# Four post-norm layers on one core: separate buffers and PSUM for the last mixer's layers, one buffer set for the third mixer's second half, one matmul pair per tile and weight pieces by block for the further tiles

## The chip, the core and the metric

The kernel is one program on one core of a Trainium2 chip. Engines: TensorE (PE; its weight loads are shown as PEld), VectorE (DVE), ScalarE (ACT), GpSimd (POOL) and SyncE (SP). Each runs its own instructions strictly in order and waits on semaphores of the others. SP, ACT and POOL also start DMA transfers; POOL alone starts the indirect ones here, in which a list of row numbers says where each of 128 rows goes or comes from. The metric is device time in microseconds (us) of one execution; "before" is the median of four runs.

## What is computed

2048 tokens (8 sequences of 256) of 128 numbers go through four layers. Each layer is a mixer and a feed-forward part (FFN), each added to its input and normalised (post-norm), in float32:

```
x = norm(x + mixer_k(x));  x = norm(x + ffn_k(x))        k = 0..3
mixer 0  recurrent scan over time          ffn 0  8 experts, 2 per token
mixer 1  latent attention, 64 latents      ffn 1  64 experts, 6 per token, and a shared one
mixer 2  gated linear attention, 4 heads   ffn 2  160 experts, 8 per token, and a shared one
mixer 3  6 layers of linear attention      ffn 3  attention with projections
         and a leaky feed-forward                 of four widths
```

Two parts matter here. Mixer 2, for each head: with c the running sum of the log gate z, o = (q k^T * exp(c_t - c_s) for s <= t) v, then a norm, a gate and a projection. FFN 2 for a token t and its eight chosen experts e, with shares p:

```
y[t] = sum over e of p[t,e] * ( silu(x[t] @ w_gate[e]) @ w_down[e] )      w_gate: 128x64, w_down: 64x128
```

## The kernel before

**Groups, halves, lanes.** The tokens are four groups g of 512 tokens. Groups 0 and 1 are the first half, 2 and 3 the second. `lanes[0]` and `lanes[1]` each own two of the eight PSUM banks (`ps`) and small buffers; group g uses lane g % 2. The expert code has the other four banks, `ps_m` (2) for gates and transposes, `ps_o` (2) for results.

**What sets the order.** The program is written stage by stage, half by half, but a tile scheduler with a timeline simulation orders the instructions of every engine: an instruction may move ahead of others of the text if its operands and buffers are free, and the queues are then fixed. Buffers come from pools; a tile with a tag has as many buffers as its pool or its `bufs` says, and a new tile of the tag waits until the oldest is no longer read. Memory of a closed pool is used again, and its new owner waits for the last reader of the old one.

**FFN 2 by tiles of 64 rows.** For one half, `plan()` turns the counts of tokens per expert into row numbers (`pl`). Each expert owns one tile of 64 rows; tokens beyond 64 go to further tiles. `place()` (L475) scatters: for each group, 4 x 8 indirect DMAs of 128 token rows from SBUF into the DRAM array `placed`, 64 per half. `routed_experts()` then works through 36 blocks of eight tiles: 20 own blocks, whose weights SP loads from the input, and 16 further blocks, whose weights first have to be laid out in the DRAM array `further`. That is done in 16 pieces: POOL gathers 128 rows of the weights into a tile `got` (L446; two buffers), SP writes it to a slice of `further`. Every further block reads a part of all 16 slices. For each block SP loads the rows (`xb`, L525) and the weights (`w`), PE transposes xb (L128), multiplies by the gate (L553), ACT and DVE apply silu (L557, L558), PE multiplies by the down weights (L571), ACT copies to `ob` and writes it to the DRAM array `made`. `xb` and `w` have two buffers. An own tile has one gate and one down matmul; in a further block both have two, with halves of the weights. `gather()` (L590) brings the rows back with 64 indirect DMAs per half, and DVE adds them, times the token's share (L487 computes the shares, inside `place()`).

**The stages in the text.** `stage(run, route, half)` runs a mixer and the routing of the next FFN for both groups of a half. Around the change the text reads:

```
stage(run, l2_route, first); plan(first); l1_experts(second)
routed_experts(first); stage(run, l2_route, second); gathers(first); plan(second)
es.close(); layers = l3_attn(ctx); run = layers(first)
routed_experts(second); gathers(second)
```

`run()` after that executes the six layers of mixer 3 for the first half, then FFN 3 for it, then both for the second half. `l2_attn` (L804) has a set of working buffers per lane. `l3_attn` (L913) loads the weights of all six layers at once (`w = [[load(...)]...]`, L917); its buffers use the memory that mixer 2's pools give back at `es.close()`. Its `layer()` has the projections L941 and L956, the attention L976 to L991 and the leaky feed-forward L1000 to L1006. One group in one of its six layers is called a group-layer here; there are 24. The memsets at L1044 to L1050 prepare tiles of FFN 3 on POOL.

## Time and profile before

| | us |
|---|---|
| median of four runs | 2382.15 |
| the four runs | 2385.47, 2378.82, 2386.44, 2376.43 |
| the profiled execution | 2375.16 |
| its span (first to last instruction) | 2373.4 |
| PE busy in it | 1836.8 |
| DVE, ACT, POOL busy | 1272.9, 958.4, 288.8 |
| mean granted PE clock | 0.83 |

The profile is of one execution. A page gives busy times by engine, the span in 40 slices (one slice is 59.3 us; each digit is the busy share in tenths), the chain of work that ended last, and groups of instructions by line. A window row gives the same for a chosen stretch: from, to, length, then the busy time and the number of instructions of PE, PEld, DVE, ACT and POOL, the granted PE clock, the busy share of the 16 DMA engines, and GB/s. A timeline row is one instruction or several of one kind: start, duration, engine, line, operation, output <- input, number, and in brackets how long the engine was idle before it and what ended that. Stages in the span: up to 980 us layers 0 and 1; to 1130 the first scatter, beside the second half of FFN 1; to 1435 the first half's blocks and the second half's mixer 2, with the second scatter from 1315; to 1548 the first gather; to 1762 the second half's blocks and the first layers of mixer 3; to 1860 the second gather; to 2373 the rest of mixer 3 and FFN 3.

### The profile page before, as it was taken

The page shows a single profiled execution, that of the slowest core. Times are in us where ns is not written, and L with a number is a line of the kernel's source. Part 1 is how long each engine was busy: PE and PEld are TensorE (multiplying, and loading weights), DVE is VectorE, ACT ScalarE, POOL GpSimd, SP SyncE. Part 2 cuts the span into 40 slices and gives each one's busy share as a digit, 9 for nine tenths or more (in the row PEclk, how much of TensorE's full clock was granted, in tenths as well). Part 3 has the DMA queues.
Part 4 walks back from the last instruction along what each step waited for, and adds up shares of the span by engine and source line. Part 5 has one row for each costly group of instructions (what it writes and reads, how often), then busy time and mean ns, then how long its engine had stood idle before and what let it go on. Part 6 is the DMA issues. An engine that isn't in the chain of part 4 may idle for free.

```text
span 2373.4 us, 48482 instructions
## 1 busy us (share of the span) xinstructions
PE 1836.8 (77%) x19224; PEld 1207.6 (51%) x19224; DVE 1272.9 (54%) x4476; ACT 958.4 (40%) x2417; POOL 288.8 (12%) x307
## 2 busy tenths in 40 slices
PE   5888879978999999846897221476774799998787
PEld 4666644544555456312585121354652566565554
DVE  3000055777877667823467221366554788566644
ACT  5667643724654365201433000143441454434413
POOL 1000000000000000172100635511025200000000
PEclk8676669989999999967799555589886899889858
DMA  2000029602324423532676243487531000000000
GB/s 85 5 4 5 5 92 274 191 11 58 96 76 116 122 63 84 171 115 86 233 221 214 91 131 123 131 273 257 177 111 39 19 1 1 1 5 5 1 1 10
DMA packets 169123, 219.78 MB, mean 93 GB/s; under 512 B 19104, under 2 KB 114848, under 8 KB 168896
## 3 DMA queue, kind: packets, MB, share of 16 engines
q1 hardware_dynamic: 145728, 164.23, 23.3%
q0 software_dynamic: 12800, 33.57, 4.6%
q10 hardware_dynamic: 10368, 18.88, 2.1%
q8 instruction: 151, 2.47, 0.4%
q14 instruction: 76, 0.62, 0.1%
HBM read 152.07 MB, written 64.55 MB: 91 GB/s over the span
## 4 chain that ended last, share of the span: by engine, by line
PE 53%; DVE 13%; DMA 9%; ACT 9%; another core or an unknown queue 7%; issue 7%; SPq 1%; POOL 1%; ACTq 0%; DVEq 0%; POOLq 0%
PE ps_o L301 6%; PE ps_m L306 6%; ACT st L248 4%; PE ps_s L239 4%; PE ps_m L311 4%; PE ps L128 3%; DMA got<-in_F_w_dram,ei 3%; PE ps L1006 2%; DMA w<-further 2%; PE ps L1000 2%; DMA further<-got 2%; PE ps_m L553 2%; PE ps L1126 2%; PE ps_s L224 2%
## 5 line engine op out<-in xcount | busy, mean ns | idle before, releaser
L308 ACT ACTIVATE h<-ps_m 128x512 f32<-128x512 f32 x196 | 116.0, 597 | 317.7 <-PE ps_m L306 211.2
L239 PE MATMUL ps_s<-st,L_a 128*32 128x16 f32 x8160 | 200.8, 206 | 44.0 <-ACT st L248 22.3
L248 ACT ACTIVATE st<-ps_s 64x32 f32<-64x32 f32 x1024 | 195.7, 191 | 90.9 <-PE ps_s L239 54.5
L301 PE MATMUL ps_o<-h,wd 128*128 128x512 f32 x384 | 206.0, 622 | 23.3 <-DVE h L314 13.2
L306 PE MATMUL ps_m<-xT,wg 128*128 128x512 f32 x384 | 203.4, 613 | 12.1 <-ACT h L308 8.7
L239 PEld LDWEIGHTS ps_s<-st,L_a 128*32 128x32 f32 x8160 | 158.1, 134 | 88.7 <-ACT st L248 73.6
L311 PE MATMUL ps_m<-xT,wu 128*128 128x512 f32 x256 | 140.6, 632 | 39.9 <-DVE junk L487 20.0
L446 POOL DMA_INDIRECT got<-in_F_w_dram,ei x32 | 31.7, 990 | 1121.9 <-DVE ei L435 969.7
L314 DVE TENSOR_TENSOR h<-h,bc 128x512 f32<-128x512 f32 x192 | 131.8, 689 | 58.7 <-ACT h L308 40.1
L571 PE MATMUL ps_o<-w,h 64*64 64x64 f32 (+1 forms) x1664 | 79.7, 274 | 104.8 <-issue 67.1
L269 DVE SCALAR_TENSOR_TENSOR outsT<-xnT,L_skip,ps 128x64 f32<-128x64 f32 x32 | 10.4, 325 | 269.6 <-PE ps L259 187.8
L590 POOL DMA_INDIRECT got<-made,pl x128 | 121.7, 951 | 230.1 <-DMA made<-ob 107.3
L475 POOL DMA_INDIRECT placed<-x,pl x128 | 124.6, 973 | 174.6 <-DVE pl L471 135.9
L553 PE MATMUL ps_m<-xg,w 128*64 128x64 f32 x1664 | 79.9, 250 | 74.9 <-DMA w<-further 29.9
L301 PEld LDWEIGHTS ps_o<-h,wd 128*128 128x128 f32 x384 | 73.3, 197 | 115.7 <-issue 67.5
L312 DVE TENSOR_TENSOR h<-h,ps_m 128x512 f32<-128x512 f32 x132 | 90.3, 684 | 76.2 <-PE ps_m L311 47.7
L571 PEld LDWEIGHTS ps_o<-w,h 64*64 64x64 f32 x1664 | 63.8, 157 | 120.7 <-issue 69.4
L557 ACT ACTIVATE h<-ps_m 128x256 f32<-128x256 f32 (+1 forms) x72 | 34.5, 480 | 222.9 <-remote 119.1
L306 PEld LDWEIGHTS ps_m<-xT,wg 128*128 128x128 f32 x384 | 72.0, 195 | 101.8 <-issue 73.2
L558 DVE SCALAR_TENSOR_TENSOR h<-h,ps_m 128x256 f32<-128x256 f32 (+1 forms) x72 | 38.5, 534 | 158.1 <-ACT h L557 90.6
L553 PEld LDWEIGHTS ps_m<-xg,w 128*64 128x64 f32 x1664 | 68.4, 159 | 96.9 <-issue 27.8
L1006 PE MATMUL ps<-A_w,hT 128*128 128x128 f32 x768 | 97.5, 281 | 18.8 <-DVE hT L1002 17.3
(357 smaller groups left out, 3796.4 us busy)
## 6 DMA issues: line engine op xcount, KB each, us to landing
bc<-comb SPq DMA_DIRECT2D x128, 256.0 KB
placed<-zero SPq DMA_DIRECT2D x72, 256.0 KB
xb<-placed SPq DMA_DIRECT2D x72, 256.0 KB
made<-ob ACTq DMA_DIRECT2D x72, 256.0 KB
further<-got SPq DMA_DIRECT2D x32, 512.0 KB
w<-further SPq DMA_DIRECT2D x32, 512.0 KB
w<-in_F_wg_dram SPq DMA_DIRECT2D x40, 256.0 KB
w<-in_F_wd_dram SPq DMA_DIRECT2D x40, 256.0 KB
```

The source lines that it names most:

```text
L239: PE.matmul(us[h][cols[c], s, u, v].rearrange("p e b -> p (e b)"), lhsT=a_sb[:, u, 4 * h + k, 32 * (c % 2) : 32 * (c % 2) + 32], rhs=prev[ ...
L248: S.activation(st[h][half, v, u, :, e, :].rearrange("p (s k) b -> p s k b", s=2), us[h][half, :, u, v, :, :], AF.Tanh,)
L301: PE.matmul(acc[g], lhsT=w, rhs=h, start=begin, stop=end, skip_group_check=True)
L306: PE.matmul(pg, lhsT=wg, rhs=xT[g], start=True, stop=True)
L308: gate = S.activation(h, pg, func).ins
L311: PE.matmul(pu, lhsT=wu, rhs=xT[g], start=True, stop=True)
L314: V.tensor_tensor(h, h, bc[:, i * GT : (i + 1) * GT], ALU.mult)
L475: i = G.indirect_dma_start(placed[h][:, :], bass.IndirectOffsetOnAxis(rw[:, j, c : c + 1], 0), x[g][:, j, :], None).ins
L553: PE.matmul(pt[half_ * TILE : (half_ + 1) * TILE, i // 2 if own else i, :], lhsT=wg[:, i, :], rhs=xg[:, i * TILE : (i + 1) * TILE], start= ...
L571: PE.matmul(out_[b * TILE : (b + 1) * TILE, c * m : (c + 1) * m], lhsT=h[k, i // 2 if own else i + b, :], rhs=wd[k, i // 2 if own else i + ...
L590: G.indirect_dma_start(got[:, c, :], None, made[g // 2][:, :], bass.IndirectOffsetOnAxis(row[g][:, j, c : c + 1], 0))
L1006: PE.matmul(po[:, j, :], lhsT=hT[:, f, j * P : (j + 1) * P], rhs=w2[:, f, :], start=(f == 0), stop=(f == 3),)
```

## The change

- **Mixer 3.** Its weights are loaded per layer, from a pool with two sets per half, instead of six sets once. It has lanes of its own (`late`), which take their PSUM from `ps_m` and `ps_o` (first half) and from the banks of `lanes` (second half). For that, `routed_experts(second)` uses the banks of `lanes`. Its buffers no longer lie in memory of mixer 2's pools: those now lie on the other side of the memory, or close with the dense experts.
- **Mixer 2.** In the second half both groups use the buffers of `lanes[0]`. The broadcast copy `zb` of z (L831, L832) is left out: the matmuls read a column of z with `to_broadcast`. The result `xb` shares the tag of `kT`.
- **Further blocks.** One gate and one down matmul per tile, as in own blocks. The weights are three DMAs, `wg` (128 x 8 runs of 256 bytes) and `wd` (2 x 64 x 4 runs of 512 bytes), instead of one of 128 x 8 runs of 512 bytes. `xb` and `w` have three buffers; `ob` is gone, the result is copied into `xb` and written from there.
- **Pieces.** They move from the end of `plan()` into `routed_experts()`: one for each of the blocks 0 to 15, its write ordered behind that block's load of `xb` on SP.
- **Scatter.** The first scatter of the second half is ordered behind the last gather of the first (without a semaphore of its own). The shares are computed by a function of their own, called after `routed_experts()`.

The core of the diff:

```diff
+    def behind(ins, other, why):
+
+        tc.add_manual_dep(
+            ins, other.name, mybir.DependencyInfo(mybir.DependencyClass.NoSync, mybir.DependencyReason.DATA), reason=why
+        )
...
-        hf, n = half[0] // 2, I["F2_w"].shape[1]
-        for k in range(16):
-            t = gp.tile([P, 8, D], F32, tag="got", name="got").rearrange("p a b -> p (a b)")
-            G.indirect_dma_start(t, None, I["F2_w"], bass.IndirectOffsetOnAxis(ei[:, k : k + 1], 0))
-            nc.sync.dma_start(out=further[hf][:, k * n : (k + 1) * n], in_=t)
+        piece_of[half[0] // 2] = ei
+
+    def lay_out(hf, k, after):
+
+        n = I["F2_w"].shape[1]
+        t = gp.tile([P, 8, D], F32, tag="got", name="got").rearrange("p a b -> p (a b)")
+        G.indirect_dma_start(t, None, I["F2_w"], bass.IndirectOffsetOnAxis(piece_of[hf][:, k : k + 1], 0))
+        behind(nc.sync.dma_start(out=further[hf][:, k * n : (k + 1) * n], in_=t).ins, after, "paced by blocks")
...
+                if not placing[h] and last_got[0] is not None:
+                    behind(i, last_got[0], "the first half goes ahead")
...
+        placed_at[g] = at, p8
+
+    def shares(ln, g):
+
+        n, k = EXPERTS, TOP
+        at, p8 = placed_at[g]
...
-    def routed_experts(half):
-
-
+    def routed_experts(half, ps_m, ps_o):
 
 
         hf = half[0] // 2
         n = TILE
         for blk in range(blocks):
             rows = slice(blk * BLOCK * TILE, (blk + 1) * BLOCK * TILE)
-            own = blk < own_blocks
-            xb = sp.tile([P, 4, D], F32, tag="xb", name="xb")
+            xb = sp.tile([P, 4, D], F32, tag="xb", name="xb", bufs=3)
             ld = nc.sync.dma_start(out=xb, in_=placed[hf][rows, :].rearrange("(p c) d -> p c d", c=4)).ins
             for i in placing[hf]:
                 tc.add_manual_dep(
                     ld, i.name, mybir.DependencyInfo(mybir.DependencyClass.Sync, mybir.DependencyReason.DATA),
                     reason="rows of the block",
                 )
-            w = sp.tile([P, BLOCK * 2 * TILE], F32, tag="w", name="w")
-            if own:
+            if blk < 16:
+                lay_out(hf, blk, ld)
+            w = sp.tile([P, BLOCK * 2 * TILE], F32, tag="w", name="w", bufs=3)
+            wg = w[:, : BLOCK * n].rearrange("p (i c) -> p i c", c=n)
+            wd = w[:, BLOCK * n :].rearrange("p (i c) -> p i c", c=D)
+            if blk < own_blocks:
                 es = slice(blk * BLOCK, (blk + 1) * BLOCK)
-                wg = w[:, : BLOCK * n].rearrange("p (i c) -> p i c", c=n)
-                wd = w[:, BLOCK * n :].rearrange("p (i c) -> p i c", c=D)
                 nc.sync.dma_start(out=wg, in_=I["F2_wg"][:, es, :])
                 nc.sync.dma_start(out=wd, in_=I["F2_wd"][:, es.start // 2 : es.stop // 2, :])
             else:
-                wt = w.rearrange("p (i c) -> p i c", c=n + TILE)
                 at = (blk - own_blocks) * BLOCK
-                nc.sync.dma_start(
-                    out=wt, in_=further[hf][at : at + BLOCK, :].rearrange("i (p c) -> p i c", p=P)
-                )
-                wg, wd = wt[:, :, :n], wt[:, :, n:]
+                f = further[hf][at : at + BLOCK, :]
+                nc.sync.dma_start(out=wg, in_=f[:, : P * n].rearrange("i (p c) -> p i c", c=n))
+                f = f[:, P * n :].rearrange("(i e) (r c) -> e r i c", e=2, c=D)
+                for e in range(2):
+                    nc.sync.dma_start(out=wd[e * n : (e + 1) * n], in_=f[e])
             xg = sp.tile([P, GT], F32, tag="xg", name="xg")
             V.tensor_copy(quarters(xg), transpose4(xb, ps_m))
-            m = GT // 2 if own else GT
-            h = sp.tile([P, GT], F32, tag="h", name="h")[:, :m]
-            pg = bank(ps_m)[:, :m]
-            pt = pg.rearrange("p (a b) -> p a b", b=TILE)
+            h = sp.tile([P, GT // 2], F32, tag="h", name="h")
+            pg = bank(ps_m)[:, : GT // 2]
+            pt = pg.rearrange("p (a b) -> p a b", b=n)
             for i in range(BLOCK):
-                for half_ in (i % 2,) if own else range(2):
-                    PE.matmul(
-                        pt[half_ * TILE : (half_ + 1) * TILE, i // 2 if own else i, :],
-                        lhsT=wg[:, i, :], rhs=xg[:, i * TILE : (i + 1) * TILE], start=True, stop=True,
-                    )
+                PE.matmul(
+                    pt[i % 2 * n : (i % 2 + 1) * n, i // 2, :],
+                    lhsT=wg[:, i, :], rhs=xg[:, i * n : (i + 1) * n], start=True, stop=True,
+                )
             S.activation(h, pg, AF.Tanh, scale=0.5)
             V.scalar_tensor_tensor(h, h, 1.0, pg, ALU.add, ALU.mult)
-            h = h.rearrange("p (a b) -> p a b", b=TILE)
-
-            po = [bank(ps_o) for _ in range(1 if own else 2)]
-            for i in range(0, BLOCK, 2):
-                for a in range(2):
-                    for b in range(2):
-
-                        if own and a != b:
-                            continue
-                        k = slice(a * TILE, (a + 1) * TILE)
-                        out_ = po[0 if own else a]
-                        c, m = i // 2, D if own else TILE
-                        PE.matmul(
-                            out_[b * TILE : (b + 1) * TILE, c * m : (c + 1) * m],
-                            lhsT=h[k, i // 2 if own else i + b, :], rhs=wd[k, i // 2 if own else i + b, :],
-                            start=True, stop=True,
-                        )
-            ob = sp.tile([P, 4, D], F32, tag="ob", name="ob")
-            if own:
-                S.copy(ob, quarters(po[0]))
-            else:
-                for a in range(2):
-                    S.copy(ob[:, :, a * TILE : (a + 1) * TILE], po[a][:, : 4 * TILE].rearrange("p (c d) -> p c d", d=TILE))
-            S.dma_start(out=made[hf][rows, :].rearrange("(p c) d -> p c d", c=4), in_=ob)
+            h = h.rearrange("p (a b) -> p a b", b=n)
+            po = quarters(bank(ps_o))
+            for i in range(BLOCK):
+                k = slice(i % 2 * n, (i % 2 + 1) * n)
+                PE.matmul(po[k, i // 2, :], lhsT=h[k, i // 2, :], rhs=wd[k, i // 2, :], start=True, stop=True)
+            S.copy(xb, po)
+            S.dma_start(out=made[hf][rows, :].rearrange("(p c) d -> p c d", c=4), in_=xb)
...
+                last_got[0] = G.indirect_dma_start(
                     got[:, c, :], None, made[g // 2][:, :], bass.IndirectOffsetOnAxis(row[g][:, j, c : c + 1], 0)
-                )
+                ).ins
...
+    def l2_attn(es, aside):
+
         H, DK, DV = 4, 32, 64
-        wp = es.enter_context(tc.tile_pool(name="a2w", bufs=1))
-        for ln in lanes:
-            ln.work = es.enter_context(tc.tile_pool(name=f"a2k{ln.i}", bufs=1))
+        wp = es.enter_context(tc.tile_pool(name="a2w", bufs=1, side="right"))
+        lanes[0].work = es.enter_context(tc.tile_pool(name="a2k0", bufs=1, side="right"))
+        lanes[1].work = aside.enter_context(tc.tile_pool(name="a2k1", bufs=1))
...
-            zb = wk.tile([P, 4, H, P], F32, tag="zb", name="zb")
-            S.copy(zb, bc_last(z, P))
...
-            xb = wk.tile([P, 4, D], F32, tag="xb", name="xb")
+            xb = wk.tile([P, 4, D], F32, tag="kT", name="xb")
...
-                    PE.matmul(pd[:, :T], lhsT=zb[:, 2 * b, h, :], rhs=tri, start=True, stop=False)
-                    PE.matmul(pd[:, P:T], lhsT=zb[:, 2 * b + 1, h, :], rhs=tri[:, :P], start=False, stop=True)
+                    PE.matmul(pd[:, :T], lhsT=z[:, 2 * b, h : h + 1].to_broadcast([P, P]), rhs=tri, start=True, stop=False)
+                    PE.matmul(pd[:, P:T], lhsT=z[:, 2 * b + 1, h : h + 1].to_broadcast([P, P]), rhs=tri[:, :P], start=False, stop=True)
...
-        w = [[load(wp, f"A3_{k}{i}") for k in ("wqv", "wk", "wo", "w1", "w2")] for i in range(DEPTH)]
...
+            wl = es.enter_context(tc.tile_pool(name=f"a3l{half[0]}", bufs=2))
             for g in half:
-                lanes[g].work = es.enter_context(tc.tile_pool(name=f"a3k{g}", bufs=1))
-            return lambda: layers(half)
-
-        def layers(half):
+                late[g].work = es.enter_context(tc.tile_pool(name=f"a3k{g}", bufs=1))
+            return lambda: layers(half, wl)
+
+        def layers(half, wl):
             y = {g: x[g] for g in half}
             for i in range(DEPTH):
+                w = [load(wl, f"A3_{k}{i}", k) for k in ("wqv", "wk", "wo", "w1", "w2")]
                 for g in half:
-                    y[g] = layer(lanes[g], g, y[g], i, *w[i])
+                    y[g] = layer(late[g], g, y[g], i, *w)
...
-            moe.enter_context(tc.tile_pool(name=k, bufs=2, space=bass.MemoryType.PSUM)) for k in ("ps_m", "ps_o")
+            ctx.enter_context(tc.tile_pool(name=k, bufs=2, space=bass.MemoryType.PSUM)) for k in ("ps_m", "ps_o")
...
-            run = l2_attn(es)
+            run = l2_attn(moe, es)
             stage(run, l2_route, first)
             plan(first)
             l1_experts(second)
-        routed_experts(first)
+        lanes[1].work = lanes[0].work
+        routed_experts(first, ps_m, ps_o)
+        for g in first:
+            shares(lanes[g % 2], g)
         stage(run, l2_route, second)
         gathers(first)
         plan(second)
-        es.close()
+
+        late = [Lane(tc, ctx, 2 + g, ps) for g, ps in enumerate((ps_m, ps_o, lanes[0].ps, lanes[1].ps))]
         layers = l3_attn(ctx)
         run = layers(first)
-        routed_experts(second)
+        routed_experts(second, lanes[0].ps, lanes[1].ps)
+        for g in second:
+            shares(lanes[g % 2], g)
         gathers(second)
-    lanes += [Lane(tc, ctx, i) for i in (2, 3)]
     last = l3_ffn(ctx)
     run()
     for g in first:
-        last(lanes[g], g, [lanes[0].ps, lanes[1].ps])
+        last(late[g], g, [ps_m, ps_o])
     layers(second)()
     for g in second:
-        last(lanes[g], g, [lanes[g].ps, lanes[g % 2].ps])
+        last(late[g], g, [late[g].ps, (ps_m, ps_o)[g % 2]])
```

## The prediction

> **What bounds the kernel now.** I read the slices of the span first, then a table of windows around the weak slices, then the chain of waits and the timeline inside them. The page:
>
> ```profile
> PE 1836.8 (77%) x19224; PEld 1207.6 (51%) x19224; DVE 1272.9 (54%) x4476; ACT 958.4 (40%) x2417; POOL 288.8 (12%) x307
> PE   5888879978999999846897221476774799998787
> POOL 1000000000000000172100635511025200000000
> ```
>
> TensorE (PE) is busy 77%, so 2373.4 - 1836.8 = 536.6 us of the span are PE idle. Wherever POOL's digits are high, PE's are low: that is where POOL issues the indirect DMAs that scatter token rows to the routed experts and gather them back. The windows (us from the start; busy us of PE, PEld, DVE, ACT, POOL; granted PE clock; DMA share; GB/s):
>
> ```profile
> 1003.00:1085.00 82.00, 36.50 (x48) 10.73 (x48) 24.36 (x93) 4.18 (x7) 62.50 (x65) 0.60 0.39 119
> 1140.00:1260.00 120.00, 111.95 (x1047) 89.31 (x1047) 65.30 (x197) 49.98 (x92) 7.50 (x8) 0.89 0.71 235
> 1260.00:1316.00 56.00, 40.82 (x723) 32.41 (x721) 47.20 (x157) 17.54 (x40) 0.74 (x1) 0.88 0.64 202
> 1316.00:1391.00 75.00, 7.55 (x99) 4.89 (x98) 8.37 (x45) 1.34 (x3) 57.02 (x60) 0.55 0.20 66
> 1391.00:1435.00 44.00, 19.84 (x338) 16.94 (x338) 17.33 (x80) 6.86 (x17) 0.44 (x1) 0.54 0.68 212
> 1435.00:1494.00 59.00, 3.98 (x31) 3.07 (x33) 10.02 (x29) 0.38 (x1) 34.23 (x36) 0.50 0.27 80
> 1494.00:1548.00 54.00, 25.34 (x216) 18.73 (x214) 20.47 (x83) 7.21 (x16) 30.22 (x32) 0.59 0.46 140
> 1660.00:1774.00 114.00, 90.39 (x1327) 72.50 (x1327) 63.21 (x203) 47.56 (x109) 8.51 (x9) 0.88 0.48 150
> 1774.00:1870.00 96.00, 49.30 (x184) 32.38 (x184) 51.69 (x234) 21.31 (x44) 52.69 (x55) 0.68 0.14 39
> ```
>
> From 1316 to 1548 PE is idle 175.3 of 232 us, a third of all its idle time: the second half's scatter, the last six blocks of the first half, then the first half's gathers with four left-over scatters. In the scatter even engines with ready work stand still, as the timeline of ACT, PE and POOL shows (start, duration, and in brackets the idle time before it):
>
> ```profile
> 1315.26 1.01 POOL L475 DMA_INDIRECT placed<-x,pl  x1 [135.93 <-DVE pl L471]
> 1382.84 0.60 ACT L557 ACTIVATE h<-ps_m 128x512 f32<-128x512 f32 x1 [57.18 <-remote]
> 1384.21 1.01 PE L571 MATMUL ps_o<-w,h 64*64 64x64 f32 x26 [54.22 <-issue]
> 1442.00 0.99 POOL L590 DMA_INDIRECT got<-made,pl  x1 [50.56 <-DMA w<-in_F_wd_dram]
> ```
>
> The scatter could start only at 1315, when the second half's row numbers (pl) were ready; the gather only at 1442, when the first half's blocks were all done. **The length of these bursts is POOL's**: 60 scatters in 1315.3 to 1391.4, 1.27 us each. By the windows PE idles 62.1 us from 980 to 1140, 23.2 to 1316, 175.3 to 1548, 50.6 to 1774 and 46.7 to 1870; 178.7 lie before and after these.
>
> **The change part by part.** The span is PE busy plus PE idle, so I sum the idle time by stage; all times are of the profiled execution (2375.2 us, span 2373.4), which is 7 us under the median of the four runs.
>
> *Pieces by block, from 980 to 1140.* Six piece gathers, each with its write, leave POOL's head, so the first scatter starts near 992 instead of 1003. The expert work of layer 1 that starves beside the scatter then ends earlier by at most those 11 us; two of four zb copies (1.90 us of ACT each) go from where PE waits for them. I take 62.1 to 56; bounds 47 (all 15) and 62.
>
> *Further blocks, tile by tile.* Before, a further block took PE 1.15 + 0.69 us, an own one 0.69 + 1.09:
>
> ```profile
> 1289.15 0.69 PE L571 MATMUL ps_o<-w,h 64*64 64x64 f32 x32
> 1291.34 1.15 PE L553 MATMUL ps_m<-xg,w 128*64 128x64 f32 x32 [0.22 <-DMA w<-further]
> 1226.80 0.69 PE L553 MATMUL ps_m<-xg,w 128*64 128x64 f32 x16
> 1227.41 1.09 PE L571 MATMUL ps_o<-w,h 64*64 64x128 f32 x16
> ```
>
> Over 32 blocks that is 2 us less PE. ACT and DVE save about 0.3 us each per block (tanh 0.60 to 0.38, h 0.68 to 0.42), beside other work: nothing. The block's weights come in 1024 runs of 256 bytes and 512 of 512, instead of 1024 of 512. From 1661 to 1762 SP's queue moved 18516 packets at 39.3% of 16 engines; taking out 13 xb loads of 128 at 102 ns (what a 2 KB packet took among own blocks) leaves 28 ns for a 512-byte run, 1.8 us per block. At the same price for a 256-byte run it is 2.7 us; at half, 1.8. Blocks follow each other every 5.4 to 6.2 us there and the DMA share is 0.48, so I take nothing. The Trainium skill, page "DMA: Bandwidth & Descriptors", section "Specifications", speaks against this edit: full rate needs at least 512 bytes, and below that the engine reads, modifies and writes. No row here has such runs among many; were each twice a 512-byte one, the load would be an estimated 4.5 us, and this sum would get up to 22 us more. xb, now held until its result is written, has three buffers for some 16 us of hold, 5.3 per block, as before.
>
> *Third mixer, one set.* g3 waits for g2's tiles, and the PE order now has g2's mixer whole, then g3's, with nearly all first-half routed blocks between them; before, both mixers ran together and the last six blocks stood behind the scatter. Work of this stage: 152.8 us of PE (1140 to 1316) + 10 before it + six blocks of 2.3 (with transposes) = 177. Its pace: the pieces, one per block, were done at 6.4 us apiece when they set the pace (16 from 1558 to 1661), so 16 x 6.4 + 4 own x 5 + 16 further x 5.4 = 209, with 5 to start: 214 from 1124, to 1338. Idle 214 - 177 = 37, against 23.2. Bounds: 15, if PE is as dense as in 1140 to 1260 (0.93); 95, if g3 starts only when g2 is done (1130 to 1266 for the pair so far, twice that). The column of z read in place of the zb copy has no row; between nothing and one more weight load for each of the 64 matmuls at 0.2 us, 13 us; I take nothing, since its other loads read the same number of values.
>
> *One burst instead of two.* With row numbers and blocks ready at about the same time, 128 indirect DMAs follow each other on POOL: 21 scatters, then gathers with scatters between, the last 21 scatters behind. The new wait holds one scatter only. The scatters are 1.27 us apart; the gathers took 97 us for 64 in 1763 to 1860, 1.5 each, since they wait for their two tiles (got). 64 x 1.27 + 64 x 1.5 = 178, plus 16 for the last blocks' results and the first xb loads (7 us from 1435 to 1442, 9 for loads), less some 8 where scatters fill the gathers' waits: 186, to about 1524. The PE order now has g0's first layer and the attention of g0's second and g1's first here, some 1.8 group-layers. A group-layer (one group through one of the six last-mixer layers) costs 16.3 us of PE: 11.7 of them are 213 of 313 us of matmul rows from 1880 to 2180, where 279 us are busy. So 29 + 13 of rest = 42 busy, 144 idle, against 175.3. That these layers can go here is what the two buffer sets and the PSUM of their own allow; before, their weights came only at 1408. Bounds: 110 (PE as busy as in the gather of 1774 to 1870, 0.51, for its last two thirds) and 180 (nothing covered).
>
> *Second half's blocks.* All 36 now run after the burst (before, nine were done by 1548), beside some 6.8 group-layers instead of five: 36 x 2.3 + 110 + 15 = 208 us of PE; pace 16 x 6.4 + 20 + 16 x 6.2 = 221. Both are near each other, so I take 238, idle 30 against 50.6. Bounds 15 and 65 (0.77 dense as now). The last-mixer weights load per half: 5 more loads for each of six layers, on a DMA with a share under 0.15 after 1774, and on SP's queue 0.3 to 0.5 us each, among block loads. What lies behind them is the next block's xb: cover is three buffers. If the cover is gone, see the second rival.
>
> *The end.* At the end of these blocks three group-layers more are done: that is the same PE work moved, and already in the sum. The gather stays 47 idle; the rest 178.7, with 5 more because less is left to lie beside the second half's last layers. shares() moves nearly nothing: its instructions keep their places in DVE's order.
>
> **Sum**: 178.7 + 5 + 56 + 37 + 144 + 30 + 47 = 497.7 us idle, against 536.6, and 2 us less PE: 41 us less, 2334 in a profiled execution, 2341 in the median.
>
> **The rivals.** *Mixers in series* (slower). Place: from 1130, PE waiting on g3 behind g2. For it: one set of buffers, and g3's projection waits for tiles that g2 reads until its end. Against: 36 blocks lie between. Price: idle 95 instead of 37, +58: 2399. It decides from g3's row numbers coming near 1386 (48 us late).
> *Last-mixer weights hold SP.* Four sets stand in SP's order among the second half's blocks, waiting for PE to be done two layers before. Three buffers cover 12 us; from 24 us per wait, 4 x 12 = 48 takes more than the gain: 2389 to 2405. For it, the chain now has A_wqv and A_wk waits at 1420; against, the wait is a whole layer old.
> *The burst stretches*: every one of the 128 at the gathers' 1.5 us, 192 + 16 = 208, 22 more: 2363. *Better cover* (110 idle in the burst, 22 where the blocks run): 42 less, 2299. *Small runs set the further pace*: 2363. *The change does less than it says*: the held scatter and shares() move little; this is in the sum.
>
> **How the numbers follow.** Chances: forecast 0.35, better cover 0.08, stretched burst 0.12, small runs 0.05, series 0.20, SP held 0.12, a sum of small losses ending within 0.3% 0.08 (0.3%, about 7 us, is what a measurement can tell from no change). Faster 0.60, same 0.08, slower 0.32. The forecast's own range is 2318 to 2364; the range from 2285 (better cover and 14 more) to 2405 takes in the series and most of SP held.
>
> **What would show it.** Right: one block of indirect DMAs on POOL, some 186 us long, starting near 1340, with last-mixer matmuls inside it; further blocks at 5.4 to 6.2 us; first scatter near 992. Wrong: a PE hole in 1130 to 1340 before a g3 line; SP loads of A_w with long waits, followed by PE waiting for xb or w; a chain full of "w<-further"; a burst over 205 us.

## The result and the profile after

The changed kernel takes 2371.14 us (median of 42 runs, 2352.27 to 2388.56); the kernel before, run beside it, 2380.26 us (63 runs, 2360.12 to 2396.27). The ratio is 0.9959, 95% interval 0.9945 to 0.9974: about 9 us faster, where the forecast had 41. The profiled execution has a span of 2367.5 us. Its page:

```profile
PE 1832.8 (77%) x18200; PEld 1199.7 (51%) x18200; DVE 1285.9 (54%) x4476; ACT 954.5 (40%) x2387; POOL 290.8 (12%) x307
PE   5888879978999999946878710368895589997787
POOL 1000000000000000171010067521003500000000
```

POOL's two hills between 1315 and 1548 have become one, and PE's digits under it are 1, 0, 3. PE idle is 2367.5 - 1832.8 = 534.7 us, practically what it was. The windows of the changed kernel by the new stages (columns as before: from, to, length, busy PE, PEld, DVE, ACT, POOL, clock, DMA share, GB/s):

```profile
997.00:1079.00 82.00, 40.71 (x62) 13.26 (x61) 28.93 (x112) 5.98 (x10) 62.78 (x64) 0.65 0.31 95
...
1130.00:1361.00 231.00, 188.17 (x1636) 148.33 (x1636) 118.45 (x349) 68.65 (x133) 13.22 (x14) 0.78 0.74 223
1361.00:1546.00 185.00, 28.13 (x104) 16.69 (x104) 60.32 (x273) 12.47 (x25) 123.49 (x128) 0.51 0.23 69
1546.00:1800.00 254.00, 211.53 (x1984) 159.93 (x1984) 168.75 (x610) 107.77 (x234) 20.53 (x23) 0.94 0.70 223
1800.00:1910.00 110.00, 55.34 (x203) 35.41 (x203) 57.88 (x250) 25.32 (x55) 60.20 (x63) 0.66 0.15 39
1910.00:2367.50 457.50, 392.00 (x2244) 262.79 (x2242) 289.47 (x1173) 184.19 (x379) 0.00 (x0) 0.88 0.04 10
```

The second half's row numbers come at 1361 (forecast 1338), the burst lasts 185 us (186), the blocks and the layers beside them end near 1800 (1338 + 186 + 238 = 1762), and the rest takes 567 us, against 611 before. Five rows of its timeline (start, duration, engine, line, idle time before) show the burst from POOL's first to last scatter, what PE did, and when SP could load the second half's first block:

```profile
1361.11 1.00 POOL L486 DMA_INDIRECT placed<-x,pl  x1 [119.12 <-DVE pl L482]
1492.53 0.45 PE L128 MATMUL ps_m<-ident,zn 128*128 128x128 f32 x1 [112.80 <-remote]
1545.12 0.97 POOL L486 DMA_INDIRECT placed<-x,pl  x1 [0.30 <-issue]
1576.56 0.33 SPq L63 DMA_DIRECT2D wqv<-in_A_wqv_dram  x1
1578.97 1.27 SPq L541 DMA_DIRECT2D xb<-placed  x3
```

PE stands still for 112.8 us until the first layer of group 0 can start; the first xb load goes out 34 us after the last scatter, behind a load of last-mixer weights. And the two longest waits of SP's queue from 1080 to 1810 (total us, times, longest):

```profile
SPq L63 <- PE ps_o L937: 166.9, 2, 162.9
SPq L541 <- DMA made<-xb: 98.2, 45, 5.2
```

The second row is new: 45 of the 72 xb loads wait until an earlier block's result has left xb. In the kernel before, the xb loads (L525) waited for the transposes instead, and the weight loads (L541) for the down matmul:

```profile
SPq L541 <- PE ps_o L571: 81.6, 25, 8.1
SPq L525 <- PE ps_m L128: 81.5, 41, 11.3
```

### The profile page after: what moved, and what is told of

It is laid out like the page before. It is cut to its first block, busy times and chain, and to the rows that moved or that the text cites. A ratio compares the mean times of both kernels' runs of the same rounds, so it can differ in the third digit from the quotient of the medians.

```text
span 2367.5 us, 46586 instructions
## 1 busy us (share of the span) xinstructions
PE 1832.8 (77%) x18200; PEld 1199.7 (51%) x18200; DVE 1285.9 (54%) x4476; ACT 954.5 (40%) x2387; POOL 290.8 (12%) x307
## 4 chain that ended last, share of the span: by engine, by line
PE 56%; DVE 13%; ACT 9%; another core or an unknown queue 8%; DMA 8%; issue 5%; SPq 1%; POOL 0%; ACTq 0%; DVEq 0%; POOLq 0%
PE ps_o L301 6%; PE ps_m L306 6%; DMA xb<-placed 5%; ACT st L248 4%; PE ps_s L239 4%; PE ps_m L311 4%; PE ps L128 3%; PE ps L1002 2%; PE ps_s L224 2%; PE ps_m L128 1%; PE ps L996 1%; PE ps L792 1%; DVE bn_st L110 1%; DMA made<-xb 1%
## 5 line engine op out<-in xcount | busy, mean ns | idle before, releaser
L128 PE MATMUL ps_m<-ident,zn 128*128 128x128 f32 x52 | 13.5, 357 | 143.5 <-remote 134.5
L311 PEld LDWEIGHTS ps_m<-xT,wu 128*128 128x128 f32 x256 | 45.2, 198 | 89.9 <-DVE junk L506 37.8
L128 PEld LDWEIGHTS ps_m<-ident,zn 128*128 128x128 f32 x52 | 7.7, 173 | 147.9 <-issue 134.5
L593 DVE SCALAR_TENSOR_TENSOR yb<-got,w,yb 128x128 f32<-128x128 f32 x128 | 44.5, 348 | 67.3 <-DMA got<-made,pl 33.3
L116 ACT ACTIVATE zn<-y,bn_off,rs_y 128x128 f32<-128x128 f32 x88 | 38.7, 489 | 95.5 <-DVE bn_off L114 58.6
L506 DVE SCALAR_TENSOR_TENSOR junk<-rt,p 128x160 f32<-128x160 f32 x128 | 44.9, 386 | 54.2 <-remote 31.6
L224 PE MATMUL ps_s<-xd,L_b 128*32 128x128 f32 x1024 | 58.0, 304 | 6.1 <-ACT xd L205 5.3
```

The source lines that it names most:

```text
L128: PE.transpose(ps[:, j, :], src[:, j, :], ident)
L224: PE.matmul(us[h][cols[c], s, u].rearrange("p t e b -> p t (e b)"), lhsT=b_sb[:, u, 4 * h + 2 * s + c // 2, 32 * (c % 2) : 32 * (c % 2) + 32],
L311: PE.matmul(pu, lhsT=wu, rhs=xT[g], start=True, stop=True)
```

## The experiments

Each ratio is to runs of the kernel before on the same chip. The chips turned out to be of two kinds. On the first, where the result above was measured, the kernel before takes about 2378 us (the runs below on chips 2, 5 and 12); on the second about 2206 us (chips 4 and 14). The kind is named with each run; ratios are set side by side within one kind only.

**Freeing xb.** The result goes into xg, which no DMA fills; xb has two buffers, xg three, the memory is the same.

```diff
-            xb = sp.tile([P, 4, D], F32, tag="xb", name="xb", bufs=3)
+            xb = sp.tile([P, 4, D], F32, tag="xb", name="xb", bufs=2)
...
-            xg = sp.tile([P, GT], F32, tag="xg", name="xg")
+            xg = sp.tile([P, GT], F32, tag="xg", name="xg", bufs=3)
...
-            S.copy(xb, po)
-            S.dma_start(out=made..., in_=xb)
+            S.copy(quarters(xg), po)
+            S.dma_start(out=made..., in_=quarters(xg))
```

> Changed kernel, with one edit: the result of a block is copied into xg instead of xb and written from there; xg has three buffers and xb two, in the same memory. So xb is free as soon as its rows are transposed. Theory C (xb held until its result is written is what slows the blocks: SP waited 98.2 us for made<-xb in 45 waits): the waits on made go, blocks of the first half end 10 to 20 us sooner, and the ratio to before is 0.986 to 0.991. Rival D (the pace is the pieces' or the weights'; the wait for made only took the place of another that ends as late): within 5 us of the changed kernel, ratio 0.994 to 0.998.

First kind: 0.9849 (0.9811 to 0.9887), and on another chip:

> Changed kernel with xg holding the result, the scatter's order as in the change. If the chip starves the other engines beside the scatter (kernel before near 2378 us): 0.982 to 0.988 again. If it does not (near 2206 us, where the changed kernel is at 1.011): freeing xb is worth the time for which blocks are held apart, 6.1 us against 4.3 in the first half, about 2.5 to 3.5 per cent, so 0.977 to 0.986.

again the first kind, 0.9815 (0.9775 to 0.9855). Against 0.9959 that is 26 to 34 us, by one buffer's use. The windows of this kernel (the first of the two):

```profile
1130.00:1300.00 170.00, 149.09 (x1623) 118.05 (x1623) 95.24 (x275) 63.44 (x127) 14.46 (x14) 0.96 0.94 304
1300.00:1540.00 240.00, 68.07 (x295) 45.00 (x294) 113.12 (x494) 36.50 (x74) 132.44 (x135) 0.62 0.19 59
1540.00:1725.00 185.00, 171.27 (x1803) 133.60 (x1803) 125.99 (x449) 85.34 (x188) 13.29 (x15) 0.97 0.92 297
1725.00:1830.00 105.00, 45.22 (x174) 30.55 (x173) 48.51 (x223) 19.88 (x42) 60.62 (x64) 0.69 0.14 40
1830.00:2334.20 504.20, 435.31 (x2276) 291.01 (x2274) 296.70 (x1214) 188.06 (x394) 0.00 (x0) 0.82 0.03 9
```

The blocks now run at a DMA share of 0.92 to 0.94 and a PE clock of 0.96. The first half's last gate matmul is at 1300 instead of 1365. From the first gate to the last the 36 blocks are 4.4 us apart, (1300 - 1145)/35, where the changed kernel has 6.3, (1365 - 1146)/35. So the pieces did not set the pace, as I had assumed: SP issues their 16 writes here from 1127.5 to 1233.8, 7.1 us apart, while 21 loads of xb go out.

The last row shows what the median hides. The second gather ends 80 us sooner than in the changed kernel (1830, not 1910), but the span is only 33 us shorter. In the part that is left PE is busy 435 us instead of 392, for nearly as many matmuls (2276, 2244), at a granted clock of 0.82 instead of 0.88. On the other chip it was the same: 499 us, 429 of them busy, at 0.84.

**How the pace goes with the number of buffers.** Two buffers instead of three, then four (with two of w instead of three, for which there was memory).

```diff
-            xb = sp.tile([P, 4, D], F32, tag="xb", name="xb", bufs=3)
+            xb = sp.tile([P, 4, D], F32, tag="xb", name="xb", bufs=2)     # or bufs=4, with w bufs=2
```

> Changed kernel, with xb in two buffers instead of three, still held until its result is written. Theory C (in the changed kernel a block follows the last by a third of the time for which xb is held, 6.85 us for some 20; freed, it was 4.3 us): with two buffers blocks are 9 to 10 us apart, the first half's blocks end 80 to 120 us later than 1380, ratio 1.04 to 1.10. Rival O (the gain with xg came from another order of the plan, not from the wait): blocks stay near 6.5 us apart, 0.995 to 1.010.

> Changed kernel, with xb in four buffers instead of three, still held until its result is written, and w in two instead of three, which the memory needs. Theory C: the hold of some 20 us is shared by four, 5 us per block; the first half's blocks end some 40 us sooner than 1380 unless two sets of weights bind, ratio 0.984 to 0.990. Rival P (two sets of weights bind as the hold did): 0.994 to 1.002.

Both ran on the second kind, so the changed kernel was run there too (below: 1.0112). Two buffers: 1.0351 (1.0324 to 1.0378); four: 0.9980 (0.9961 to 1.0000). The expected ratios were those of the first kind and are missed; the pace decides. First and last gate matmul of the first half, timeline of the changed kernel on this kind of chip, of two buffers, and of four:

```profile
1096.45 0.69 PE L569 MATMUL ps_m<-xg,w 128*64 128x64 f32 x16
1316.00 1.12 PE L569 MATMUL ps_m<-xg,w 128*64 128x64 f32 x16
```

```profile
1091.15 0.69 PE L569 MATMUL ps_m<-xg,w 128*64 128x64 f32 x16
1371.69 1.12 PE L569 MATMUL ps_m<-xg,w 128*64 128x64 f32 x16 [0.79 <-DVE xg L564]
```

```profile
1092.53 0.69 PE L569 MATMUL ps_m<-xg,w 128*64 128x64 f32 x16
1283.38 0.69 PE L569 MATMUL ps_m<-xg,w 128*64 128x64 f32 x16 [0.74 <-DMA w<-further]
```

Over 35 steps: 8.0 us with two, 6.3 with three, 5.5 with four; freed, 4.4. The steps times the buffers, an estimate of the hold as long as the wait for made sets the pace, are 16, 19 and 22 us (with four, w had a buffer less as well). The wait for made sets the pace of the changed kernel on both kinds of chip; with two buffers the steps are 8.0 us, not the 9 to 10 that I expected. Why the estimate grows with the buffers no run looked into.

**The hold alone, in the kernel before.** ob is made the same tile as xb, with three buffers.

```diff
-            ob = sp.tile([P, 4, D], F32, tag="ob", name="ob")
+            ob = xb        # and xb with bufs=3
```

> Kernel before, with one edit: ob is gone, the result of a block is copied into xb and written from it, and xb has three buffers, as in the change. Theory C (holding xb until its result is written costs time by itself; in the changed kernel, freeing it moved the time from 0.996 to 0.985 of before): the kernel before becomes slower, ratio 1.005 to 1.015, with waits of SP on made before xb loads. Rival I (the hold only costs beside the changed order of mixers and pieces): 0.997 to 1.003.

First kind: 0.9997 (0.9966 to 1.0028). SP waits 174.4 us for made in its trace, and the median does not move, as rival I had it. But the blocks do get slower: the first 17 of the first half are 7.2 us apart instead of 5.5, and the last gather goes out at 1902 instead of 1859. Of these 43 us 29 are won back behind it, in a part of 485 us instead of 515 (this execution is 12 us above its median). So the hold comes with slower blocks in this kernel too, and the end does not show it; why the last part is shorter no run separates.

**Small runs.** The weights of a further block come in one DMA again, with runs of 512 bytes; the kernel leaves out the order of the rows that the matmuls need, so the values of the further tiles are not right, while the number and shapes of the matmuls are the same.

```diff
-                nc.sync.dma_start(out=wg, ...)
-                for e in range(2):
-                    nc.sync.dma_start(out=wd[e * n : (e + 1) * n], in_=f[e])
+                nc.sync.dma_start(out=w.rearrange("p (i c) -> p i c", c=n + TILE), in_=f.rearrange("i (p c) -> p i c", p=P))
```

> Changed kernel, with one edit: the weights of a further block are loaded by one DMA of 1024 runs of 512 bytes, as the kernel before did, into the same tile. The matmuls then read rows in an order that is not theirs, so the values of the further tiles are wrong; their number and shapes are the same. Theory E (runs of 256 bytes and three DMAs for one slow the further blocks): further blocks come 0.5 us or more closer together, 16 to 30 us less in all, ratio 0.983 to 0.990. Rival F (hidden: the load lands in about 4.4 us while blocks are 6 us apart): within 5 us of the changed kernel, ratio 0.994 to 0.998.

> Changed kernel with xg holding the result (xg three buffers, xb two), and with the further weights loaded in one DMA of 1024 runs of 512 bytes (their values are then in the wrong order, number and shapes of the matmuls the same). With the wait for made gone, the load of the weights could be the next limit. Theory E' (small runs are the next limit): 0.972 to 0.980 against 0.985 with small runs. Rival F' (still hidden): 0.982 to 0.988.

First kind: 0.9981 (0.9959 to 1.0002), and with xb freed 0.9889 (0.9848 to 0.9931). Neither is faster than with 256-byte runs (0.9959; 0.9849 and 0.9815). The runs of 256 bytes cost nothing that these runs show. Their price, from SP's queue in the changed kernel, 1705 to 1785 (packets, MB, share of 16 engines):

```profile
q1 hardware_dynamic: 27099, 12.83, 63.3%
```

63.3% of 16 x 80 us is 810 us; less 1941 packets of 2 KB at 102 ns, 612 us are left for 25158 packets, 24 ns each. With two thirds of them 256 bytes and 28 ns for a 512-byte one, that is an estimate of 22 ns for 256 bytes: dearer per byte, but far from twice a longer run.

**Pieces back in plan().** The loop over 16 pieces stands again at the end of plan(), the call in the blocks is gone.

```diff
+        for k in range(16):
+            ... G.indirect_dma_start(t, None, I["F2_w"], ...); nc.sync.dma_start(out=further[hf]..., in_=t)
...
-            if blk < 16:
-                lay_out(hf, blk, ld)
```

> Changed kernel, with one edit undone: the 16 pieces of a half stand at the end of plan() again, as in the kernel before, instead of one per block. Theory G (pieces one per block set the pace of the own blocks, 6.85 us each from 1138 to 1275 against about 5.7 before, since SP waits for each piece to land with block loads behind it): own blocks of the first half come 1 us closer, row numbers of the second half 10 to 20 us sooner, ratio 0.986 to 0.992. Rival H (pieces at the head delay the scatter by as much): the first scatter starts 6 to 11 us later, the own blocks gain that back, ratio 0.993 to 0.999.

First kind: 1.0048 (1.0023 to 1.0073), slower than the changed kernel by 0.9%. Both theories miss. The own blocks start at 1156 instead of 1146; first-half blocks are 5.6 us apart and gates end at 1354 instead of 1365. The row numbers come as before, at 1363 instead of 1361, but POOL's order now has 16 gathers ahead of the first scatter (1384). The last scatter goes out at 1543 (1545), so the gain is gone by then, and the loss comes behind it: the second half's gate matmuls run from 1607 to 1832 instead of 1587 to 1790. Pieces by block are worth some 20 us here; why those blocks start later and go slower no run separates.

**The third mixer's part alone, in the kernel before.** One set for the second half, zb replaced, with the tags that belong to it.

```diff
+        lanes[1].work = lanes[0].work
         routed_experts(first)
...
-            zb = wk.tile([P, 4, H, P], F32, tag="zb", name="zb")
-            S.copy(zb, bc_last(z, P))
...
-                    PE.matmul(pd[:, :T], lhsT=zb[:, 2 * b, h, :], ...)
+                    PE.matmul(pd[:, :T], lhsT=z[:, 2 * b, h : h + 1].to_broadcast([P, P]), ...)
```

> Kernel before, with the change's part in the third mixer alone: in the second half both groups use one buffer set, zb is replaced by a column of z read with to_broadcast, the result shares kT's tag, the routing has tiles of its own. Theory J (one set makes the second half's mixers run in a row, but the 36 blocks fill the gaps; the row numbers come later and the first half's blocks earlier): row numbers 20 to 45 us later than 1315, the blocks end before the scatter instead of after it, and the time is within 0.993 to 1.003. Rival K (two mixers in a row leave PE idle, the price of my series rival): row numbers past 1386 and a ratio over 1.01.

First kind: 0.9993 (0.9970 to 1.0016). The timeline of POOL, the first gather of the first half and the first scatter of the second:

```profile
1333.58 0.95 POOL L590 DMA_INDIRECT got<-made,pl  x1 [159.33 <-DMA made<-ob]
...
1393.16 1.00 POOL L475 DMA_INDIRECT placed<-x,pl  x1 [0.30 <-issue]
```

The scatter goes out 78 us later than before (1393, not 1315), but it waits for nothing then (0.30 us behind the gather ahead of it): the row numbers of the two groups were ready at 1383 and 1386, 68 us later than before. That is the point from which my series rival was to make the kernel slower, and it isn't slower: the blocks are done some 100 us earlier, so that the gather (at 1334 instead of 1442) fills the time in which POOL waits for row numbers.

**SP held by weights.** The loads of layers 2 to 5 for the first half are ordered behind block loads.

```diff
+                then = block_ld[1][5 + 10 * (i - 2)] if half[0] == 0 and i > 1 else None
-                w = [load(wl, f"A3_{k}{i}", k) for k in (...)]
+                w = [load(wl, f"A3_{k}{i}", k, then) for k in (...)]
```

> Changed kernel, with one edit: the loads of the last mixer's weights for layers 2 to 5 of the first half are ordered on SP behind the second half's block loads of xb number 5, 15, 25 and 35, so that no weight load that waits for PE stands ahead of the first xb load. Nothing else of the text differs. Theory A (SP held: in the changed kernel SP waits for 162.9 us on a wqv load until 1576, and the first xb load of the second half goes out at 1579 though the last scatter was issued at 1545): the first xb load goes out near 1550, the second half's blocks end 15 to 30 us sooner, ratio to before 0.984 to 0.990. Rival B (PE had the last mixer's layers to do meanwhile, and the stage is bound by PE, which was busy 211 of 254 us): the blocks start sooner but end at the same time, ratio 0.994 to 0.998.

> Changed kernel with xg holding the result, all scatters held, and the last mixer's weights from layer 2 on ordered on SP behind block loads. With xg and the held scatters alone the first xb load of the second half went out 70 us after the last scatter on a starving chip and 2 us after it on the other. Theory A (SP held costs): 5 to 15 us less on a starving chip (0.962 to 0.967), nothing on the other (0.973 to 0.978). Rival B (PE's own order puts the layers first, so that an early load is not used; with xb held, this edit made the kernel 0.9 per cent slower): no better than 0.969 or 0.975, or worse.

First kind: 1.0048 (1.0016 to 1.0081), and with xb freed and scatters held 0.9730 (0.9684 to 0.9775), beside 0.9687 without the edit. The timeline of the first of the two, SP and PE:

```profile
1548.00 2.38 SPq L544 DMA_DIRECT2D xb<-placed  x2
...
1584.20 0.69 PE L573 MATMUL ps<-xg,w 128*64 128x64 f32 x16
```

The xb load goes out 31 us sooner, the first gate matmul at 1584 instead of 1587: PE's order has the layers of groups 0 and 1 ahead of it. The hold of SP is real, but without it the first gate comes only 3 us sooner. Why the edit makes the end worse I did not settle; its last part, from 1910, takes 474 us against 457, with PE busy 408 against 392 at a granted clock of 0.85 against 0.88.

**The order of the burst.** All scatters of the second half behind the first half's last gather, or all ahead of its first.

```diff
-                if not placing[h] and last_got[0] is not None:
+                if last_got[0] is not None:
                     behind(i, last_got[0], "the first half goes ahead")
```

For the other order this line goes, and every gather of groups 0 and 1 is put behind the last scatter:

```diff
+                if g < 2:
+                    behind(last_got[0], placing[1][-1], "the second half's rows go ahead")
```

> Changed kernel with xg holding the result, and with every scatter of the second half ordered behind the last gather of the first, not only its first one. The gathers of groups 0 and 1 then run before all 64 scatters. Theory L (the burst's PE idle falls when g0's and g1's first layers can run while scatters are issued): PE idle in the burst is 20 to 30 us less than with the mixed order, ratio 0.974 to 0.981. Rival M (layers beside the scatters starve, and the second half's blocks start later): 0.985 to 0.995.

First kind, with xb freed: 0.9687 (0.9649 to 0.9726), the best of all. But the theory's cover is not what does it, as the windows of this kernel show:

```profile
1130.00:1310.00 180.00, 160.22 (x1666) 126.16 (x1667) 100.98 (x298) 65.14 (x129) 13.17 (x14) 0.92 0.91 292
1310.00:1404.00 94.00, 9.90 (x29) 5.79 (x28) 63.61 (x292) 3.99 (x9) 63.21 (x65) 0.54 0.20 57
1404.00:1484.00 80.00, 8.46 (x28) 5.89 (x28) 13.33 (x65) 5.66 (x12) 60.91 (x63) 0.51 0.18 62
...
1850.00:2306.00 456.00, 392.78 (x2250) 262.01 (x2250) 294.54 (x1178) 185.08 (x382) 0.00 (x0) 0.89 0.03 10
```

PE is busy 18 of the 174 us of the burst. Total PE idle is 510 us, 7 more than with xb freed alone; PE busy is 1796 instead of 1831, at a mean clock of 0.846 instead of 0.833. The gain over xb freed alone lies in PE's busy time, and there in the last part: the second gather ends 20 us later (1850, not 1830), but 456 us follow instead of 504, at a granted clock of 0.89 instead of 0.82. On what the granted clock depends there stays open.

> Changed kernel, with one edit: every scatter of the second half is ordered behind the last gather of the first, not only its first one; xb is held until its result is written, as in the change. Theory L (gathers first, so that g0 and g1 are ready before the scatters; it gave 0.969 against 0.985 where xg holds the result): the same 1.2 to 1.8 per cent here, ratio 0.978 to 0.984. Rival N (it works only where the blocks are done early, at 1300 instead of 1380, so that the gathers fill the time before the row numbers of the second half come): 0.992 to 1.002.

> Changed kernel with xg holding the result, and the other order of the burst: all 64 scatters of the second half first, every gather of the first half ordered behind them. Theory Q (the second half's blocks then run while the gathers are issued, as in the kernel before, where nine were done by then; the blocks' matmuls need no gather): PE idle in the burst falls, 0.975 to 0.983. Rival R (POOL waits for the row numbers from 1300 to 1350 with gathers ready, and g0's layers come last): 0.988 to 1.000.

These two fell on the second kind: 1.0104 (1.0064 to 1.0144) and 0.9859 (0.9826 to 0.9893). So both were run again beside the changed kernel and the best version:

> The changed kernel itself, beside the three runs below. The last runs (all scatters held; xb in two buffers; xb in four; scatters first) were on another chip, where the kernel before takes 2204 us instead of 2378, and where PE was busy 68 of 82 us in the first scatter instead of 41. Theory S (the starving of all engines beside the scatter belongs to some chips, not to the kernel): if this chip is like that one, PE is again busy 65 to 70 of 82 us in the first scatter and the changed kernel takes 2210 to 2250, a ratio of 1.00 to 1.02, since the gain forecast for covering the burst is not there to be had; if it is like the first ones, 40 to 43 of 82 us and 0.994 to 0.998.

> Changed kernel with every scatter of the second half held behind the last gather of the first, xb held until its result is written. On a chip where the scatter starves the others: theory L says 0.978 to 0.984, rival N (gathers first pays only when the blocks are done early) 0.992 to 1.002. On a chip where it does not: 1.006 to 1.014, as measured before.

> Changed kernel with xg holding the result and all 64 scatters of the second half ahead of the first half's gathers. On a chip where the scatter starves the others: theory Q (the second half's blocks run beside the gathers) 0.975 to 0.983, rival R (POOL waits for row numbers with gathers ready) 0.988 to 1.000. On a chip where it does not: 0.983 to 0.989, as measured before.

> Changed kernel with xg holding the result and all scatters of the second half behind the first half's gathers, 0.969 where the scatter starves the others; 0.966 to 0.972 again there. Where it does not, the burst has less to give and the blocks are as fast: 0.980 to 0.992.

Again the second kind: changed kernel 1.0112 (1.0082 to 1.0142), scatters held 1.0121 (1.0092 to 1.0149), xb freed with scatters first 0.9866 (0.9839 to 0.9893), xb freed with scatters held 0.9754 (0.9728 to 0.9779). The window of the first scatter in the changed kernel on this kind:

```profile
1000.00:1082.00 82.00, 68.89 (x179) 33.22 (x177) 54.63 (x216) 22.34 (x39) 62.50 (x63) 0.88 0.51 153
```

The same 64 DMAs, issued as fast, leave PE 69 of 82 us instead of 41, with three times PE's instructions done. Theory S holds. It is no matter of one trace: in this scatter PE is busy 37 to 42 us in all twelve traces of the first kind and 63 to 69 in all eight of the second. The scatter of the second half shows it again, in the kernel with xb freed and scatters held, whose row for the first kind stands above (1404 to 1484, 8.46 us of PE); on the second kind:

```profile
1345.00:1425.00 80.00, 53.46 (x240) 37.56 (x240) 49.98 (x210) 31.32 (x70) 60.80 (x64) 0.78 0.19 64
```

Holding the scatters without freeing xb does nothing on this kind (rival N); on the first kind it was not run without xg. With xb freed, gathers first beats scatters first.

## Why the prediction was half right

The time lies in the range, and on the first kind of chip the direction was right, and so was the mechanism in its outline: two bursts became one, three group-layers moved ahead, the end is 44 us shorter. The size was a quarter of the forecast. The forecast was worked out from a trace of the first kind; on the second the same change is 1.1% slower, which no term of it foresaw. The sum was made of PE idle by stage, so it can be checked term by term (us; the stages end where the windows above do):

| stage | before | forecast | after | xb freed |
|---|---|---|---|---|
| first scatter | 62.1 | 56 | 53.6 | 52.5 |
| second mixers, first half's blocks | 23.2 | 37 | 42.8 | 20.9 |
| burst | 175.3 | 144 | 156.9 | 171.9 |
| second half's blocks | 50.6 | 30 | 42.5 | 13.7 |
| gather | 46.7 | 47 | 54.7 | 59.8 |
| the rest | 178.7 | 183.7 | 184.2 | 184.2 |
| sum | 536.6 | 497.7 | 534.7 | 503.0 |

The changed kernel is idle for 37 us more than forecast: 18 in the two stages of blocks and 21 in the burst and the gather, less 2 elsewhere.

- **Step that failed: "xb, now held until its result is written, has three buffers for some 16 us of hold, 5.3 per block, as before".** It was costed at nothing, by a comparison with the old pace. Measured, the pace is 6.3 us, by the estimate above a hold of 19, and what it has to be compared with is the pace that the change makes possible, 4.4 us. Freed, the two stages of blocks lose 51 us of idle time; 20 come back in the burst and the gather. The sum is then 503, near the forecast of 498, and the ratio 0.982 to 0.985 where the forecast is 0.983, but that is in part luck: the blocks' stages are 32 us under the forecast, the burst and the gather 41 over.
- **"the pieces, one per block, were done at 6.4 us apiece when they set the pace"** was wrong with it, as a pace for blocks. With xb free the pieces' writes are 7.1 us apart and the blocks 4.4. The changed kernel shows 6.3, near my number, for another reason.
- **"29 + 13 of rest = 42 busy" in the burst**: 28. The burst's length was right (185, 186). Group 0's first layer has its input only after its 32 gathers, the last of them at 1449, and the additions and norm behind them; PE waits 112.8 us, to 1492, and has 53 us of the burst left.
- **Gather**: 55 instead of 47; no run looked into it.
- **What the sum does not see**: it takes PE's busy time as fixed. In total it nearly is (1833 us, with xb freed 1831), but a stage's busy time moves with the granted clock: of the 80 us that freeing xb has won at the end of the second gather, 47 are lost behind it, where the clock is 0.82 instead of 0.88.
- Right: the scatter starts at 997 (992), PE busy 1832.8 (1834.8), small runs cost nothing, so that the rule of the Trainium skill, page "DMA: Bandwidth & Descriptors", section "Specifications", with its 512 bytes for full rate, does not decide here; the column of z costs nothing that shows (513 ns a matmul at a clock of 0.78, zb's 439 at 0.89; the shortest take 379 in both). That shares() and the one held scatter move little is not shown: no run takes them out by themselves.
- The rival "mixers in series" did not come true: the row numbers come at 1361, not near its 1386. With the mixer's part alone they do come at 1383 to 1386, and the time does not move, as POOL gathers meanwhile. "SP held" came true at one place, for 34 us, and cost no more than 3 us there, as PE had layers ahead. Neither made the kernel slower on the first kind.

## What to carry to other kernels

When a copy through a spare buffer is saved by writing back into the loaded tile, price the hold as hold time over buffers, and compare it with the pace that the rest of the change is to reach, not with the old one: here the saved buffer ate three quarters of the gain, while the same edit did not move the old kernel's time. A result can often go into a tile that no transfer fills, in the same memory. And before a stall of a trace is taken as a law, see it on a second chip.

## What the runs showed of the hardware

On some chips a run of indirect DMAs from POOL starves the other engines, on others far less: in the same 82 us of 64 scatters PE is busy 41 us or 69, DVE 29 or 55, ACT 6 or 22, while POOL issues one every 1.3 us on both. The kernel before takes 2378 us on the one kind and 2206 on the other, and the sign of the change differs, 0.9959 and 1.0112. What makes the difference between the chips no run here shows. A change that rearranges such bursts has no one size; the version with xb freed and scatters held is faster on both, 0.9687 and 0.9754.
